# A spectral layer's four filters: row tiles, wider moving operands and more result buffers

## The chip, the cores and the metric

The kernel runs on one core of a Trainium2 chip. A core has a matrix engine (TensorE, PE in the profile, with its weight loads listed apart as PEld), a vector engine (VectorE, DVE), a scalar engine (ScalarE, ACT), a general engine (GpSimd, POOL) and a queue engine (SyncE, SP). The metric is the device time in microseconds, the median of several runs, lower is better. One further execution was recorded by the hardware profiler; every duration in this text comes from that record.

## The reference, cut to what matters

The program sends eight images of 64 x 64 points with 96 channels through four layers. The first three are state-space layers (two of the selective kind, one chunked) and take most of the time. The change is in the fourth, the spectral layer:

```
xu = upsample(x)                      # 64x64 -> 128x128, a low-pass filter along h and along w
h  = xu @ W1.T + b1                   # 96 -> 384, at each of 128*128 points
h  = coef0 + coef1*h + coef2*h*h
h  = h @ W2.T + b2                    # 384 -> 96
out = lowpass(h)[:, :, ::2, ::2]      # 128x128 -> 64x64, along h and along w
x  = x + out                          # x goes in through a group norm
```

Both filters are products of one matrix along h and the same matrix along w: `up` (64 to 128) and `down` (128 to 64). All arithmetic is in float32.

## The kernel before, in words

The eight images are worked off one after the other by the loop at the end of the program. For each one, three layers are run, and then `spectral_layer` (called in the last line of that loop). This function has five stages, each of which needs all of the one before it:

1. **Turn in.** `xs` (96 channels by 4096 points) is loaded in four pieces, GpSimd applies the group norm into `xn` (L1101), and 64 transposes (L1108), one for each row h, put w on the partitions. VectorE copies four rows at a time to `xt` (L1111), 64 partitions.
2. **Up along w.** For each of the 96 channels one matmul (L1116) has `xt[:, :, c]` as its stationary operand (64 partitions, 64 columns, 384 bytes from column to column) and `up` as its moving operand (64 rows, 128 columns). Four channels share a PSUM bank; VectorE (L1121) and ScalarE (L1119) empty the banks in turn into `x1`: h on 64 partitions, then 128 places of w, then channels.
3. **The main loop**, 32 iterations of four places of w each. Four matmuls go up along h (L1130: stationary `x1[:, w, :]`, 64 rows by 96 columns, moving `up`, 128 columns). ScalarE copies the result to `x2` (L1132), three matmuls apply W1 (L1136, 512 moving columns), ScalarE and VectorE form the polynomial (L1139, L1146), twelve matmuls apply W2 (L1153: a contiguous stationary block of 128 x 128, 96 moving columns), and VectorE adds the bias into `g` (L1160), which has h on 128 partitions.
4. **Down along h.** For each channel one matmul (L1169) with the stationary operand `g[:, :, c]`, 128 rows by 128 columns, 384 bytes from column to column, and the moving operand `down`, 64 columns. Eight channels fill a bank; VectorE (L1174) and ScalarE (L1172) empty the banks in turn into `g2`.
5. **Turn out.** For each of 16 tiles of four rows: one matmul goes down along w (L1178), four transposes bring the layer's input back (L1181), ScalarE copies these to `res` (L1185), VectorE adds the matmul (L1186), and SP writes `res` to HBM (L1187). `res` has two buffers, so the copy for tile n waits until the write of tile n-2 has landed.

A float32 matmul stands in the trace as two weight loads and two matmul records; a transpose as one of each. Within a stage a scheduler of the framework decides the order of instructions on each engine: matmuls of the next iterations' L1130 are threaded between L1136 and L1153, so that a group of L1130 can be cut into pieces. The state-space layers have orders written out by hand and are not touched. The next image starts with transposes (L1223) of a tile `tok` that is loaded (L1217) into memory which the spectral layer has used, so these loads are issued after its last transposes.

## Time and profile before

| | us |
|---|---|
| median of 3 runs (lowest, highest) | 31217.13 (31208.32, 31267.33) |
| the profiled execution's own time | 31126.95 |
| its span, first to last instruction | 31125.2 |
| PE busy, share of the span | 24477.4 (79%) |
| DVE busy | 24790.2 (80%) |
| POOL busy | 21609.0 (69%) |
| ACT busy | 16342.4 (53%) |

The last image's spectral layer, by stage, from the timeline:

| stage | from | to | us |
|---|---|---|---|
| turn in, from the first transpose | 30799.69 | 30809.55 | 9.9 |
| up along w | 30809.55 | 30831.53 | 22.0 |
| main loop | 30832.62 | 31049.21 | 216.6 |
| down along h | 31049.96 | 31091.95 | 42.0 |
| turn out, to the end of the span | 31091.75 | 31125.2 | 33.5 |

How to read the profile: a group's row gives busy time, the mean ns of one instruction, and after the second bar the time that the engine sat idle before it, with what ended the wait. Matmuls overlap, so the mean of one is longer than the distance from one to the next. A shape such as 64*128 before the tile sizes is rows by columns of the stationary operand. PEclk is the clock that was granted to TensorE, as a share of full speed; in this trace it is 1.00 or 0.50 at any moment.

### The profile page before, as it was taken

What the parts mean: (1) busy time and instruction counts of PE and PEld (TensorE: products, weight loads), DVE (VectorE), ACT (ScalarE), POOL (GpSimd) and SP (SyncE); (2) the same over time, 40 slices, a digit from 0 to 9 for tenths busy, and PEclk for the clock granted to TensorE, in tenths of its full rate; (3) what the DMA queues carried; (4) which work ended last, traced back from release to release, by engine and by line L of the source; (5) the groups of instructions that cost most, each with busy time, mean ns of one, the idle gap of its engine ahead of it and who ended that gap; (6) DMA issues with size and microseconds to landing.
All of it is one profiled execution on the core that took longest, in us unless ns stands there. A gap on an engine that the chain in (4) does not pass through costs nothing. (4 is left out here: it accounts for less than half of the span.)

```text
span 31125.2 us, 279248 instructions
## 1 busy us (share of the span) xinstructions
PE 24477.4 (79%) x90246; PEld 9300.6 (30%) x90246; DVE 24790.2 (80%) x17921; ACT 16342.4 (53%) x28493; POOL 21609.0 (69%) x8844
## 2 busy tenths in 40 slices
PE   7797877978779787797877978779787797877978
PEld 1241422414225132241412414124141241412414
DVE  9859688596885968859698596985969859698596
ACT  5536455364553645536455364653646536465364
POOL 8739487395873958739587394973948739487394
PEclk7777776777777777777777777777777777776777
DMA  5315253052530525305253152531525315253152
GB/s 124 90 24 131 64 120 92 23 133 64 119 93 21 131 67 120 92 23 132 64 122 89 25 132 63 123 88 28 133 59 123 88 27 132 60 123 88 27 132 62
DMA packets 1503971, 2689.39 MB, mean 86 GB/s; under 512 B 305624, under 2 KB 313144, under 8 KB 1502512
## 3 DMA queue, kind: packets, MB, share of 16 engines
q1 hardware_dynamic: 1485872, 2665.23, 36.6%
q8 instruction: 722, 11.83, 0.2%
q10 hardware_dynamic: 16640, 6.29, 0.1%
q14 instruction: 737, 6.04, 0.1%
HBM read 2287.51 MB, written 383.06 MB: 86 GB/s over the span
## 5 line engine op out<-in xcount | busy, mean ns | idle before, releaser
L569 DVE TENSOR_TENSOR_SCAN h<-da,db 128x1026 f32<-128x1026 f32 x6144 | 13727.8, 2280 | 513.0 <-PE py L607 173.9
L590 POOL TENSOR_TENSOR h<-h,c 128x2048 f32<-128x2048 f32 x3072 | 12755.2, 4183 | 148.4 <-ACT state L585 144.5
L533 PE MATMUL pu<-du,cst 32*128 32x512 f32 x4096 | 3239.1, 881 | 3525.3 <-DVE db L539 3493.7
L554 ACT ACTIVATE da<-dx,a0s 128x512 f32<-128x512 f32 x6144 | 4235.3, 690 | 2600.4 <-DVE h L569 2440.4
L554 ACT ACTIVATE da<-dx,a2s 128x512 f32<-128x512 f32 x6144 | 4234.5, 690 | 2591.4 <-DVE h L569 2432.0
L607 PE MATMUL py<-h,cst 128*32 128x512 f32 x24576 | 5432.2, 814 | 68.3 <-POOL h L590 68.0
L539 POOL TENSOR_TENSOR db<-du,b 128x2048 f32<-128x2048 f32 x1024 | 4657.7, 4549 | 580.8 <-ACT db L525 580.8
L539 DVE TENSOR_TENSOR db<-pu,b 128x2048 f32<-128x2048 f32 x2048 | 4637.4, 2264 | 6.3 <-issue 6.3
L607 PEld LDWEIGHTS py<-h,cst 128*32 128x32 f32 x24576 | 1182.6, 145 | 4982.1 <-issue 4505.5
L533 PEld LDWEIGHTS pu<-du,cst 32*128 32x128 f32 x4096 | 802.3, 243 | 5542.4 <-DVE db L539 3998.6
L229 POOL TENSOR_SCALAR xn<-xs,sb 96x512 f32<-96x512 f32 x192 | 208.0, 1088 | 3179.8 <-DVE sb L209 3038.8
L455 PE MATMUL pv<-u,wk 96*128 96x512 f32 x2048 | 1765.1, 1003 | 759.0 <-ACT raw L451 759.0
L952 ACT ACTIVATE sg<-sg 128x768 f32<-128x768 f32 x1024 | 819.2, 800 | 2422.4 <-PE sg L936 2422.4
L883 POOL TENSOR_TENSOR rr<-lr,cc 128x768 f32<-128x768 f32 x256 | 435.9, 1703 | 2266.9 <-ACT lr L881 1177.4
L446 PE MATMUL pv<-u,wk 96*96 96x512 f32 x2048 | 1475.4, 849 | 501.1 <-ACT state L585 239.4
L597 PE MATMUL py<-y,cst 96*96 96x512 f32 x1536 | 1551.2, 1108 | 394.6 <-ACT raw L460 356.7
L498 POOL TENSOR_TENSOR du<-raw,u 96x512 f32<-96x512 f32 x1024 | 1445.7, 1438 | 0.0
L984 DVE TENSOR_TENSOR wt<-wt,cbm 128x768 f32<-128x768 f32 x1024 | 1091.0, 1085 | 344.5 <-ACT wt L953 341.2
L585 ACT COPY state<-h 128x4 f32<-128x4 f32 x3072 | 604.6, 197 | 1163.9 <-DVE h L569 1163.8
L1022 PE MATMUL py<-wt,xdt 128*32 128x128 f32 x12288 | 1017.0, 331 | 233.2 <-DVE y L1060 155.0
L1146 DVE SCALAR_TENSOR_TENSOR f<-p,w3bs,f 128x512 f32<-128x512 f32 x768 | 576.4, 751 | 718.6 <-ACT f L1139 691.8
L1030 PE MATMUL py<-ce,state 96*96 96x128 f32 x3968 | 1115.4, 371 | 0.0
(210 smaller groups left out, 32236.4 us busy)
## 6 DMA issues: line engine op xcount, KB each, us to landing
dx<-dd SPq DMA_DIRECT2D x4096, 192.0 KB, 3.8
b<-bcd SPq DMA_DIRECT2D x2048, 256.0 KB, 5.2
c<-bcd SPq DMA_DIRECT2D x2048, 256.0 KB, 6.5
du<-dud SPq DMA_DIRECT2D x2048, 128.0 KB, 2.7
dd<-raw SPq DMA_DIRECT2D x1024, 192.0 KB, 5.3
dud<-du SPq DMA_DIRECT2D x512, 128.0 KB, 1.9
xd<-xs SPq DMA_DIRECT2D x256, 192.0 KB, 2.1
xs<-xd SPq DMA_DIRECT2D x128, 384.0 KB, 5.8
```

The costliest lines, as they stand in the source:

```text
L446: nc.tensor.matmul(pv[:DM], weights[k][:, hi, 128:], uv[hi], start=(hi == 0), stop=(hi == 1))
L455: nc.tensor.matmul(pv, weights[k][:, hi, :128], uv[hi], start=(hi == 0), stop=(hi == 1))
L498: nc.gpsimd.tensor_mul(cut(du[:, hf, :], wh), cut(delta[hf], wh), uv[hf])
L533: nc.tensor.matmul(pu, sel[rows, :], m["du"][rows, n // 3, :], start=True, stop=True)
L539: (nc.gpsimd if pool else nc.vector).tensor_mul(groups(m["db", n]), (m["du2"][:, n // 3, :] if pool else m["pu"]) .unsqueeze(1) .to_broadc ...
L554: nc.scalar.activation(dst[:, g, :LC], made[i]["dx"][n // 3][:, n % 3, :], AF.Exp, scale=av4[:, k, n, gs : gs + 1],)
L569: nc.vector.tensor_tensor_scan(made[i]["h", n][:, at][:, way], das[p][:, rev : 2 * SEG + rev][:, way], made[i]["db", n][:, at][:, way], 0. ...
L590: nc.gpsimd.tensor_mul(h, h, made[i]["c"])
L597: nc.tensor.matmul(py, skip[:, hf, :] if k == 0 else ident[:DM, :DM], view((u if k == 0 else y)[:, hf, :], wh, c * LC, LC), start=True, st ...
L607: nc.tensor.matmul(py[32 * q : 32 * q + 32, :], red, hs[q][:, g, :], start=False, stop=(g == NSG - 1),)
L984: nc.vector.tensor_mul(it["wt"], it["wt"], m["cbm"][:, j : j + 1, :].to_broadcast([128, RK, Q]),)
L1030: nc.tensor.matmul(py[:, i, hf, :], it["before"][:, 96 * hf : 96 * hf + 96], m["ce"][:, j, :], start=False, stop=True,)
```

## The change

- **Turn in.** Each transpose takes 128 points (its own row and the next), so that `xt` has 128 partitions, of which the upper 64 hold the next row. `xn` gets 64 more columns of zeros for the last one.
- **Up along w.** The moving operand is `up0`: 128 rows, the lower 64 `up` and the upper 64 zero, so the product is the same. `x1` becomes 128 partitions by 64 places: w from 0 to 63 on partitions 0 to 63, w from 64 to 127 on partitions 64 to 127. Each PSUM bank is emptied in two halves, VectorE the first and ScalarE the second; in the built program ScalarE's half waits for VectorE's.
- **Up along h.** The loop takes places 4n of the lower half and 64+4n of the upper half as a pair. Their eight matmuls alternate between rows 0 to 63 and rows 64 to 127 of the array, into two PSUM tiles out of three. The table of constants holds `up` twice, once for each half of the partitions.
- **Down along h.** The moving operand is `down2`, `down` written twice, 128 columns; the second half of the product is not used. A bank holds four channels instead of eight, and there are 24 copies of 256 elements instead of 12 of 512.
- **Turn out.** `res` has five buffers instead of two.

```diff
-            up, down = filters[:64, :128], filters[:, 128:]
-            xn = lp.tile([DM, L], F32, name="xn")
-            xt = lp.tile([64, 64, DM], F32, name="xt", tag="turn")
-            x1 = lp.tile([64, 128, DM], F32, name="x1")
+            up, down = filters[:, :128], filters[:, 128:]
+
+            down2 = lp.tile([128, 2, 64], F32, name="down2")
+            nc.gpsimd.tensor_copy(down2, down.unsqueeze(1).to_broadcast([128, 2, 64]))
+            up0 = lp.tile([128, 128], F32, name="up0")
+            nc.gpsimd.memset(up0[64:], 0.0)
+            nc.gpsimd.tensor_copy(up0[:64], up[:64])
+            xn = lp.tile([DM, L + 64], F32, name="xn")
+            nc.gpsimd.memset(xn[:, L:], 0.0)
+
+            xt = lp.tile([128, 64, DM], F32, name="xt", tag="turn")
+
+            x1 = lp.tile([128, 64, DM], F32, name="x1")
...
-                    pt = pp.tile([64, 4, DM], F32, name="pt", tag="t")
+                    pt = pp.tile([128, 4, DM], F32, name="pt", tag="t")
                     for i in range(4):
                         nc.tensor.transpose(
-                            pt[:, i, :], xn[:, (h0 + i) * 64 : (h0 + i) * 64 + 64], ident[:DM, :DM]
+                            pt[:, i, :], xn[:, (h0 + i) * 64 : (h0 + i) * 64 + 128], ident[:DM, :DM]
                         )
...
-                        nc.tensor.matmul(pt[:, i, :], xt[:, :, c0 + i], up, start=True, stop=True)
+                        nc.tensor.matmul(pt[:, i, :], xt[:, :, c0 + i], up0, start=True, stop=True)
                     dv = x1[:, :, c0 : c0 + 4].rearrange("p w c -> p c w")
-                    if c0 % 8:
-                        nc.scalar.copy(dv, pt)
-                    else:
-                        nc.vector.tensor_copy(dv, pt)
+                    nc.vector.tensor_copy(dv[:64], pt[:, :, :64])
+                    nc.scalar.copy(dv[64:], pt[:, :, 64:])
...
-                for w0_ in range(0, 128, 4):
-
-                    p2 = pp.tile([DM, 4, 128], F32, name="p2")
-                    for i in range(4):
-                        nc.tensor.matmul(p2[:, i, :], x1[:, w0_ + i, :], up, start=True, stop=True)
+                for n in range(32):
+                    w0_ = 4 * (n // 2) + 64 * (n % 2)
+                    if n % 2 == 0:
+
+                        p2s = [pp.tile([DM, 4, 128], F32, name="p2", bufs=3) for _ in range(2)]
+                        for i in range(4):
+                            for j in range(2):
+                                rows = slice(64 * j, 64 * j + 64)
+                                nc.tensor.matmul(
+                                    p2s[j][:, i, :],
+                                    x1[rows, w0_ + i, :],
+                                    up[rows],
+                                    start=True,
+                                    stop=True,
+                                )
+                    p2 = p2s[n % 2]
...
-                for c0 in range(0, DM, 8):
-                    p5 = pp.tile([128, 8, 64], F32, name="p5")
-                    for i in range(8):
-                        nc.tensor.matmul(p5[:, i, :], g[:, :, c0 + i], down, start=True, stop=True)
-                    dv = g2[:, :, c0 : c0 + 8].rearrange("p h c -> p c h")
-                    if c0 % 16:
-                        nc.scalar.copy(dv, p5)
+                for c0 in range(0, DM, 4):
+                    p5 = pp.tile([128, 4, 2, 64], F32, name="p5")
+                    for i in range(4):
+                        nc.tensor.matmul(
+                            p5[:, i, :, :], g[:, :, c0 + i], down2, start=True, stop=True
+                        )
+                    dv = g2[:, :, c0 : c0 + 4].rearrange("p h c -> p c h")
+                    if c0 % 8:
+                        nc.scalar.copy(dv, p5[:, :, 0, :])
                     else:
-                        nc.vector.tensor_copy(dv, p5)
+                        nc.vector.tensor_copy(dv, p5[:, :, 0, :])
...
-                    res = sp.tile([64, 4, DM], F32, name="res")
+                    res = rp.tile([64, 4, DM], F32, name="res")
...
-    c[:64, K_UP : K_UP + 128] = 2 * low_up[:, ::2].T
+    c[:, K_UP : K_UP + 128] = np.tile(2 * low_up[:, ::2].T, (2, 1))
```

(`rp` is a new pool, `spec4`, with five buffers.)

More of the change, by code (lines that the diff above doesn't have):

```diff
@@ L1162, in spectral_layer @@
                     )
-            with tc.tile_pool(name="ps2", bufs=3, space=PSUM) as pp:
+            with (
+                tc.tile_pool(name="ps2", bufs=3, space=PSUM) as pp,
+                tc.tile_pool(name="spec4", bufs=5) as rp,
+            ):
                 g2 = lp.tile([128, 64, DM], F32, name="g2", tag="turn")
-                for c0 in range(0, DM, 8):
-                    p5 = pp.tile([128, 8, 64], F32, name="p5")
-                    for i in range(8):
-                        nc.tensor.matmul(p5[:, i, :], g[:, :, c0 + i], down, start=True, stop=True)
-                    dv = g2[:, :, c0 : c0 + 8].rearrange("p h c -> p c h")
-                    if c0 % 16:
-                        nc.scalar.copy(dv, p5)
+                for c0 in range(0, DM, 4):
[7 more added lines that the diff above has]
+                        nc.scalar.copy(dv, p5[:, :, 0, :])
                     else:
-                        nc.vector.tensor_copy(dv, p5)
+                        nc.vector.tensor_copy(dv, p5[:, :, 0, :])
                 for h0 in range(0, 64, 4):
```

## The prediction

> **What bounds the kernel now.** I read first where the changed lines stand: the groups by line put the lines of `spectral_layer` in eight stretches of 325 to 345 us, one per image, about 8.6% of the span; nothing else can gain or lose directly. Then the stretch table of the last image (length; busy time and count of PE, PEld, DVE, ACT, POOL; granted clock; DMA share; GB/s):

> ```profile
> 30799.70:30804.00 4.30, 4.30 (x27) 4.30 (x28) 2.98 (x6) 0.00 (x0) 4.30 (x6) 0.50 0.49 122
> 30809.60:30831.50 21.90, 21.90 (x192) 21.73 (x192) 12.10 (x12) 11.07 (x11) 0.00 (x0) 1.00 0.00 1
> 30832.60:30839.70 7.10, 7.08 (x21) 4.74 (x22) 0.75 (x1) 1.94 (x3) 0.00 (x0) 0.52 0.00 0
> 30839.70:31049.20 209.50, 207.92 (x1197) 150.42 (x1195) 88.60 (x126) 90.52 (x125) 0.00 (x0) 1.00 0.00 1
> 31051.40:31091.70 40.30, 40.30 (x187) 40.30 (x187) 6.08 (x6) 5.11 (x5) 0.00 (x0) 0.50 0.00 0
> ```

> PE fills every stage up to the turn out, DVE and ACT are half idle: PE's pace is the layer's pace, and the clock is part of it. The down stage runs at half clock; so does the start of the main loop. The timeline shows that up along w has two speeds:

> ```profile
> 3596.60 40.12 PE L1116 MATMUL pt<-filters,xt 64*64 64x128 f32 x192 [1.34 <-DVE xt L1111]
> 11397.97 21.98 PE L1116 MATMUL pt<-filters,xt 64*64 64x128 f32 x192 [1.34 <-DVE xt L1111]
> ```

> Over the eight images: 40.1, 40.2, 22.0, 22.0, 22.0, 39.9, 38.9, 22.0; mean 30.9 us. Third, single lines. In two short windows of full clock, the strided weight load of L1169 and the contiguous one of L1153, both 128x128, and in another two row groups side by side in an untouched layer:

> ```profile
> L1169 PEld LDWEIGHTS p<-filters,g x6: 292/310/310, 31049.9 to 31051.0; 128*128 128x128 f32 x6
> L1153 PEld LDWEIGHTS p<-w3bs,f x362: 186/192/193, 3700.2 to 3799.3; 128*128 128x128 f32 x181
> L936 PE MATMUL sg<-rr,lr x8: 481/481/585, 5998.1 to 5999.1; 32*128 32x384 f32 x8
> ```

> L1169's loads start every 0.217 us (six in 1.1 us) at full clock, and the stage keeps 42.0/192 = 0.218 at half clock: the load sets that pace, not the matmul. L936's eight records of 384 columns, 0.32 us each if alone, all start within 1.1 us: two rows of four. Last, the turn out waits for its own writes:

> ```profile
> 31110.85 0.47 ACT L1185 COPY res<-p 64x384 f32<-64x384 f32 x1 [2.21 <-DMA out_dram<-res]
> 31111.56 0.47 ACT L1185 COPY res<-p 64x384 f32<-64x384 f32 x1 [0.23 <-DMA out_dram<-res]
> ```

> **Durations.** L1136's records of 512 columns follow at 0.43 us at full and 0.85 at half clock (its weight loads at 30850.55, 30850.98; 30837.03, 30837.88). So streaming takes 0.84 or 1.67 ns a column: 128 columns 0.107 or 0.213, 96 columns 0.080 or 0.160, 64 columns 0.054 or 0.107 us.

> [...] L1116 agrees (64 strided columns load in 193 ns, as long as L1153's 128). [...] a block of six L1130 records takes 0.83 us, where 6 x 0.11 is 0.66.

> **The change, per image.**

> *Turn in.* At half clock a transpose now loads 128 columns (0.213) and streams 96 (0.160): 64 x 0.213 = 13.6 us, plus 0.9 to the last copy, 14.5; before, first transpose to first L1116 took 9.66 on average, set by DVE's 16 copies of 0.557. Its share is 0.160/0.213 x 0.75 = 0.56, which I take as not waking. Loss 4.8. If it wakes, DVE sets the pace again and the loss is about 1. The GpSimd sets and copies stand before `xn`, where GpSimd is idle, or end under the transposes: nothing; uncovered, 128 columns cost under 0.77 (L1101's 512).

> *Up along w.* 128 rows, streaming 0.213 of 0.213: wakes within one or two windows, on average after 4.3 us, 20 records; the other 172 at 0.1145 give 19.7. Together 24.0 against 30.9: gain 6.9. The two half copies: L1121's 512 elements took 1.02; taking 0.15 as fixed, 256 take 0.58, ACT the same, 1.2 in series but spread over four banks, period 0.91: hidden. ACT's last copy now waits for DVE's: loss 0.4.

> *Start of the main loop.* Sixteen L1130 and six L1136 records at half clock took 3.5 + 4.7 us; at full clock 1.75 + 2.6. The array now arrives awake: gain 4.0.

> *Pairs.* In a cycle of four iterations L1130's five blocks take 1.47 + 0.83 + 0.60 + 0.83 + 0.60 = 4.33 us, 6.5 for six iterations. In the built order of the new kernel six iterations have five blocks. Counting neighbours of different halves as one step of 0.22, they have 4, 3, 1, 3 and 4 steps (the scheduler leaves some matmuls of one half in a row): 15 x 0.22 + 5 x 0.17 = 4.15. With 0.35 for fewer cuts in L1153, 2.7 in six iterations, 14 in 32. Bounds: 0 without overlap, 16. ACT has 2.9 us of work in an iteration of some 6: it does not become the bound.

> *Down along h.* Streaming is 0.107 under a load of 0.217, hidden; at half clock 0.213, hidden too. Pace stays, 41.7 us. The share is now 0.49 at full clock: it keeps it, which shows only later. Bounds: if load and stream did not overlap, +10; if the pace were the stream's, 192 x 0.115 = 22, a gain of 20. I take +0.4 for the shorter last copy.

> *Turn out.* From the first L1181 to the next image's L1223: 33.8 us on average (last image 33.5 to the end). Where no write is waited for, a tile takes 1.24 us of PE. With five buffers a write has 6.2 us, it needs 3.9 from copy to landing (0.5 + 0.6 + 0.6 + 2.2): no wait. Last transposes after some 20.2; then `tok` is issued and lands 5.8 later (median 5.3, 5.8 in the first image): 26.3. Gain 7.5, last image 20.2 + 1.6 + 0.6 + 2.2 = 24.7, gain 8.8. What was late because of writes is next late because of `tok`.

> Sum: 8 x (-4.8 + 6.9 - 0.4 + 4.0 + 14 + 0.4) = 161, and 61 from the turn out: **222 us**. Against the profiled execution's own time 31126.95 that is 30905.

> The median of the runs shown is 90 above that execution. Four of its images went up along w awake; were all eight asleep, it would be 72 more. If runs differ by this, the new kernel, which has one speed there, does not carry the difference; if by something else, it carries 90. I take the middle, 42: **30947**.

> **Rivals.**
> (1) *The down stage halves.* If the 0.217 belongs to the half-empty stream, 128 columns give 22 us: 20 x 8 = 160 more, 30787. Against it: the pace is the same at both clocks and the load itself lasts 310 ns.
> (2) *No overlap in the pairs*, by [...] a new wait in the scheduler's order: the 112 fall to about 0, 31059. Against it: L936.
> (3) *The transposes wake the array*: +30, 30917; inside my range.
> (4) *Slower: the main loop falls asleep.* Paired row tiles might count as 64 rows. Its stretch at full clock has PE busy 99%, and half clock would double it: the gain of 222/8 = 28 us is gone when work of 28 us in each main loop runs asleep; all 198 asleep would be 8 x 198 = 1584 more than the forecast, 32531. Against it: L1136 and L1153 alone give (2.58 x 0.75 + 24 x 0.080)/6.2 = 0.62, far above what puts to sleep.

> **How the numbers follow.** A change below 0.2%, 62 us, is about what a measurement of this kernel can't tell from none. My forecast with (3): 0.68, from 30850 to 31040. (1) 0.12; (2) 0.10; (4) 0.05; gains that cancel to near nothing 0.05. The range must reach (1) and (2): 30780 to 31095. Faster 0.90 (forecast, 1, 2), same 0.05, slower 0.05.

> **What would show it.** After the change the row of L1116's successor should have 24 us in every image with the clock at 0.50 for its first few us; the transposes 13.6 us at 0.50 (right) or under 11 with a rise (wrong); the paired matmuls two records starting together, main loop about 198 us; down 41.7 us at clock 1.00 (a figure near 22 would refute the strided load); no wait of ACT on `out_dram`, and L1223's successor waiting for a DMA. The forecast fails if the pairs run in series or the down stage is bound by something else.

## The result, and the profile after

The median went from 31212.72 us (four runs) to 30974.42 us (four runs): 238 us less, ratio 0.9926 with a 95% interval of 0.9908 to 0.9943. A second comparison, made later beside the kernel before, gave 31133.32 and 30939.07 us, ratio 0.9940 (0.9923 to 0.9957). The forecast was 30947 us. (One of the timed runs of a kernel shown below, "g for contiguous loads", took 38871 us at a mean granted clock of 0.65 instead of 0.74 and is left out of its median.) The sum is close; two of its terms were far off in opposite directions, which only the stages show.

The profiled execution took 30955.91 us (span 30953.8). The stretch table of its last image, with the same columns as the one of the kernel before (start and end; length; busy time and count of PE, PEld, DVE, ACT, POOL; granted clock; DMA share; GB/s). The six rows are turn in, up along w, start of the main loop, the rest of it, down along h, turn out:

```profile
30646.40:30655.70 9.30, 7.90 (x65) 7.24 (x65) 7.92 (x16) 0.00 (x0) 5.65 (x9) 0.81 0.22 58
30655.70:30677.70 22.00, 21.95 (x192) 21.76 (x192) 13.44 (x24) 13.04 (x23) 0.00 (x0) 1.00 0.01 1
30679.00:30686.10 7.10, 7.03 (x39) 4.13 (x40) 2.60 (x4) 4.26 (x7) 0.00 (x0) 1.00 0.00 0
30686.10:30886.70 200.60, 192.78 (x1179) 136.69 (x1178) 86.78 (x125) 88.07 (x122) 0.00 (x0) 1.00 0.00 1
30887.50:30929.90 42.40, 42.40 (x195) 42.40 (x196) 7.12 (x12) 6.49 (x12) 0.00 (x0) 1.00 0.01 1
30929.90:30953.80 23.90, 19.60 (x96) 7.82 (x93) 8.75 (x16) 7.98 (x17) 0.00 (x0) 1.00 0.28 67
```

The clock rises within the transposes, 3.7 us after the first, and from there it is full (1.00) to the end of the layer. In the 200.6 us of the main loop PE is busy 192.78: it now idles 7.8 us, where before it idled 1.6 in 209.5. Down along h takes its 42.4 us at full clock too.

The stages of all eight images, from the first record of a stage to that of the next, as means over the images (the gain is before minus after, times eight; the forecast's sums stand beside it):

| stage | before, us per image | after | gain x 8 | forecast x 8 |
|---|---|---|---|---|
| turn in | 9.67 | 9.88 | -2 | -38 |
| up along w | 30.87 | 21.95 | +71 | +55 |
| gap to the main loop | 1.10 | 1.28 | -1 | -3 |
| main loop | 217.04 | 207.72 | +75 | +144 |
| down along h, with the gap before it | 42.53 | 43.03 | -4 | +3 |
| turn out | 33.70 | 26.17 | +60 | +61 |
| the layer | 334.91 | 310.02 | +199 | +222 |

Outside the layer the two executions differ by 28 us the other way (28446 and 28474). Nothing in the changed lines touches that time; below it is seen to vary between executions of one kernel.

Single lines answer to those of before. In the timeline, the turn in and up along w of the second image:

```profile
7452.31 8.09 PE L1117 MATMUL pt<-cst,xn 96*128 96x96 f32 x64 [5.40 <-POOL xn L1110]
7461.80 21.95 PE L1125 MATMUL pt<-up,xt 128*64 128x128 f32 x192 [1.40 <-DVE xt L1120]
```

The 64 transposes take 8.1 us here and 7.9 to 8.9 over the images, not 13.6. The line view of the transposes and of the strided load of down along h, first image (durations are smallest, median, largest in ns):

```profile
L1117 PE MATMUL pt<-cst,xn x64: 246/364/419, 3572.6 to 3581.1; 96*128 96x96 f32 x64
...
L1190 PEld LDWEIGHTS p<-down,g x189: 292/313/313, 3814.4 to 3855.7; 128*128 128x128 f32 x189
```

And the timeline of ACT in the last turn out, with the wait of the next image's first transpose from the list of waits of the first turn out:

```profile
30947.23 0.47 ACT L1208 COPY res<-p 64x384 f32<-64x384 f32 x1 [0.77 <-PE p L1204]
30948.47 0.47 ACT L1208 COPY res<-p 64x384 f32<-64x384 f32 x1 [0.77 <-PE p L1204]
30949.71 0.47 ACT L1208 COPY res<-p 64x384 f32<-64x384 f32 x1 [0.77 <-PE p L1204]
...
PE pt L1246 <- DMA tok<-in_x_dram: 6.2, 1, 6.2
```

The copies come every 1.24 us and wait for PE, never for a write; in the first turn out PE then waits 6.2 us for `tok`. This is the forecast's picture of the turn out.

**Where the main loop's gain went.** The groups by line of PE, for one main loop of the kernel before (an image whose up along w was at full clock), then of the kernel after. After the bar stands idle time just before the group, and what ended it:

```profile
L1153 PE MATMUL p<-w3bs,f 128*128 128x96 f32 x768 | 100.9, 276 | 1.2 <-DVE f L1146 1.0
L1136 PE MATMUL p<-x,w3as 96*128 96x512 f32 x192 | 97.6, 619 | 0.3 <-ACT x L1132 0.3
L1130 PE MATMUL p<-filters,x 64*96 64x128 f32 x256 | 38.4, 289 | 1.1 <-ACT x L1119 1.1
```

```profile
L1171 PE MATMUL p<-w3bs,f 128*128 128x96 f32 x768 | 99.5, 276 | 6.8 <-DVE f L1164 6.3
L1154 PE MATMUL p<-x,w3as 96*128 96x512 f32 x192 | 95.5, 606 | 1.1 <-ACT x L1150 0.7
L1141 PE MATMUL p<-filters,x 64*96 64x128 f32 x256 | 23.5, 283 | 1.3 <-ACT x L1128 1.3
```

Up along h is 15 us shorter on PE (part of that is the clock at its start, 0.52 before and 1.00 after), and W2 now waits 6.3 us for `f`, the polynomial's result, which it multiplies. The timeline of PE shows one such place:

```profile
3704.68 1.05 PE L1154 MATMUL p<-x,w3as 96*128 96x512 f32 x2
3705.56 0.58 PE L1171 MATMUL p<-w3bs,f 128*128 128x96 f32 x4
3706.08 0.90 PE L1141 MATMUL p<-filters,x 64*96 64x128 f32 x12
3707.38 2.47 PE L1171 MATMUL p<-w3bs,f 128*128 128x96 f32 x20 [0.41 <-DVE f L1164]
```

L1154's last matmul makes the third part of `f` possible; ScalarE (0.78 us) and VectorE (0.75 us) must work on it before the twenty records of L1171 can run. In between PE has only four records of W2 and the paired block. The block is shorter than it was, by just the overlap that was wanted, and so PE arrives 0.41 us too early. The twelve L1141 records take up 0.9 us here; twelve at 0.11 would have taken 1.3.

### The profile page after: what moved, and what is told of

It is laid out like the page before. It is cut to its first block, busy times and chain, and to the rows that moved or that the text cites. A ratio compares the mean times of both kernels' runs of the same rounds, so it can differ in the third digit from the quotient of the medians.

```text
span 30953.8 us, 279486 instructions
## 1 busy us (share of the span) xinstructions
PE 24269.9 (78%) x90246; PEld 9118.0 (29%) x90246; DVE 24825.8 (80%) x18065; ACT 16387.8 (53%) x28637; POOL 21617.7 (70%) x8876
## 5 line engine op out<-in xcount | busy, mean ns | idle before, releaser
L455 PEld LDWEIGHTS pv<-u,wk 96*128 96x128 f32 x2048 | 534.9, 289 | 1918.2 <-ACT raw L451 1442.4
## 6 DMA issues: line engine op xcount, KB each, us to landing
b<-bcd SPq DMA_DIRECT2D x2048, 256.0 KB, 5.2
c<-bcd SPq DMA_DIRECT2D x2048, 256.0 KB, 6.5
```

Source lines behind the costliest of these rows:

```text
L455: nc.tensor.matmul(pv, weights[k][:, hi, :128], uv[hi], start=(hi == 0), stop=(hi == 1))
```

## The experiments

For each main loop I give below what a line's records *own*: the time from a record's start to the next record's start, without the idle time between them, added up. This counts overlapped records once.

**Pairs undone.** Only up along h is changed back; the scheduler orders it anew.

```
-    p2s = [pp.tile([DM, 4, 128], F32, name="p2", bufs=3) for _ in range(2)]   (for n % 2 == 0)
-    for i in range(4):
-        for j in range(2): matmul(p2s[j][:, i, :], x1[64*j:64*j+64, w0_ + i, :], up[64*j:64*j+64])
+    rows = slice(64 * (n % 2), 64 * (n % 2) + 64)
+    p2 = pp.tile([DM, 4, 128], F32, name="p2", bufs=2)
+    for i in range(4):
+        matmul(p2[:, i, :], x1[rows, 4 * (n // 2) + i, :], up[rows])
```

> Pairs alone undone: each tile's four up-along-h matmuls stand together again, on its own 64 rows, with two p2 buffers as before; all else as in the changed kernel. Theory (W: the pairs save some 11 us of TensorE in each main loop, and 6.3 us of that come back as a wait for f): the L1141 records own 34 instead of 23.1 us, TensorE's idle time in the main loop falls from 7.8 to under 2 us, the loop goes from 207.7 to about 213, the whole kernel about 40 us slower than the changed one. Rival (A: row tiles overlap only a little on the array, the wait is an accident): the idle time stays near 7.8, the loop grows by what the array saved alone. Second rival (N: the pairs save nothing, all of the loop's gain was the clock): loop 207.7, no difference.

Measured: 30925.61 us, ratio to the kernel before 0.9928 (0.9912 to 0.9944), as good as the changed kernel's. The main loop took 209.4 us in four images and 210.9 to 214.3 in the four in which the clock fell to one half about 2 us after its start, for 3.4 to 10.2 us (in the profiles of both kernels every stretch at one clock lasts a window of 3.413 us or a whole number of them; one at half clock is a "lost window" from here on); mean 210.8 against 207.7. The groups of PE in the first main loop:

```profile
L1163 PE MATMUL p<-w3bs,f 128*128 128x96 f32 x762 | 100.3, 276 | 2.1 <-DVE f L1156 1.0
L1146 PE MATMUL p<-x,w3as 96*128 96x512 f32 x192 | 95.7, 608 | 0.5 <-ACT x L1142 0.5
L1138 PE MATMUL p<-filters,x 64*96 64x128 f32 x256 | 30.8, 288 | 1.3 <-ACT x L1128 1.3
```

The wait for `f` falls from 6.3 to 1.0 us, as theory W wanted, and PE's idle time from 7.8 to 2.7. But the L1138 records own only 29.2 us, not 34: even without pairs, some of their time is gone. In the trace, where the block of one tile (rows 0 to 63) ends and that of the next (rows 64 to 127) begins, the two overlap by themselves. The blocks stand in the same order as in the kernel before, of 12, 6, 4, 6 and 4 records; but one of 12 owns 1.19 us instead of 1.48, and one of 6 owns 0.60 or 0.67 instead of 0.82. So the pairs as written are worth 6.0 us on PE and lose 5.2 of them to idle time; with a change of 0.8 in W1 and W2 together, 1.7 us a loop remain, less than a measurement of the whole can see. (Summed over the images with the lost windows, the layer took 2504 us instead of 2480; outside the layer this execution happened to spend 62 us less.)

**The order written by hand.** The same work; the order of the main loop is written out instead of left to the scheduler.

```
+    fa = first(xa)                       # first: W1 and f of a tile; second: W2 and bias
+    for k in range(16):
+        fb = first(xb)
+        if k < 15:
+            p2s = rows_up(k + 1)         # eight matmuls, halves alternating
+            xa = to_sbuf(p2s[0])
+        second(fa, 4 * k)
+        if k < 15:
+            xb = to_sbuf(p2s[1])
+            fa = first(xa)
+        second(fb, 4 * k + 64)
```

> Same work as in the changed kernel, but the main loop's order is written out by hand: W1 of one tile always stands between the W1 of the tile before and that tile's W2, and eight paired matmuls, strictly alternating, follow each second W1. So f has a whole W1 (2.6 us) more to be ready. Theory W: no wait for f is left; 192 x 0.43 + 768 x 0.112 = 168.5 us, 16 blocks of 8 x 0.11 + 0.17 = 16.8, some 8 for changes between lines as now, 2 for the start: about 195 us instead of 207.7, the whole kernel about 100 us faster than the changed one. Rival A (overlap is limited by the array): the wait goes, but the paired blocks own more than 20 us again and the loop stays above 201. Rival S (the scheduler's order is not what costs; the wait only moves to x2 or p3): idle time stays above 5 us, loop within 2 us of 207.7.

Measured: 30826.06 us, ratio 0.9897 (0.9876 to 0.9918). The main loop took 189.2 us, or 190.9 to 192.4 in three images that lost one or two windows; mean 190.2, which is 17.6 us less than after. Theory W had put it at about 195. The groups of PE and its timeline:

```profile
L1177 PE MATMUL p<-w3bs,f 128*128 128x96 f32 x761 | 90.7, 276 | 0.0
L1158 PE MATMUL p<-x,w3as 96*128 96x512 f32 x192 | 88.6, 598 | 0.7 <-ACT x L1151 0.7
L1140 PE MATMUL p<-filters,x 64*96 64x128 f32 x256 | 17.9, 279 | 1.3 <-ACT x L1128 1.3
```

```profile
3684.82 2.82 PE L1177 MATMUL p<-w3bs,f 128*128 128x96 f32 x24
3687.48 2.77 PE L1158 MATMUL p<-x,w3as 96*128 96x512 f32 x6
3690.17 1.12 PE L1140 MATMUL p<-filters,x 64*96 64x128 f32 x16
3691.22 2.92 PE L1177 MATMUL p<-w3bs,f 128*128 128x96 f32 x24
```

No wait for `f` is left. Of the 18.5 us between 207.7 and 189.2, 7.1 are idle time, 6.3 are L1140 (23.1 to 16.8 owned), and 2.6 and 2.5 are W1 and W2, which are no longer cut into pieces of one and two records. Rivals A and S fall.

**The same order, halves not alternating.**

```
-    for i in range(4):
-        for j in range(2):
+    for j in range(2):
+        for i in range(4):
```

> The hand-written order of the run before it, but in each block the four matmuls of the first row half stand together, then the four of the second: no neighbour is of another half, except at the change. Theory W: overlap is lost, 16 blocks grow by 8 x 0.11 less one overlap, about 0.85 us each, so the loop is 13 to 15 us longer than with alternating halves (about 209), the whole kernel some 110 us slower than that. Rival A: difference of 5 us a loop or less. Together with the run before it this gives the pairs' own worth with no wait in the way.

Measured: 30860.17 us, ratio 0.9904 (0.9889 to 0.9919); loop 196.9 us where no window was lost, 7.7 more than with alternating halves. The up along h lines own 25.0 instead of 16.8, which is 8.2 more, and 0.5 of idle time is gone. 7.7 is between the theory's 13 to 15 and rival A's 5; the whole kernel is 34 us slower than with alternating halves, not 110. The starts of the sixteen records of one block, in us from its first, in the order in which each half was issued (the two halves are told apart by their own even steps of 0.109):

```
rows 0 to 63:    0     0.186 0.296 0.405 0.514 0.623 0.732 0.841
rows 64 to 127:  0.520 0.706 0.816 0.925 1.034 1.143 1.252 1.361
```

The first record of the second half starts while the first half still has three to go. So TensorE took work of the other half three to four records early: neighbours need not alternate to overlap, here it was enough that they lay within that reach. That is also part of why undoing the pairs cost so little.

**g for contiguous loads.** The array that down along h loads is turned round.

```
-    g = lp.tile([128, 128, DM], F32, name="g")
+    g = lp.tile([128, DM, 128], F32, name="g")
...
-    g[:, w0_ : w0_ + 4, :], p4, ...
+    g[:, :, w0_ : w0_ + 4].rearrange("p c w -> p w c"), p4, ...
...
-    nc.tensor.matmul(p5[:, i, :, :], g[:, :, c0 + i], down2, ...)
+    nc.tensor.matmul(p5[:, i, :, :], g[:, c0 + i, :], down2, ...)
```

> The changed kernel with g laid out so that the 128 elements which a down-along-h weight load reads in a partition stand next to one another (g is [128, channel, w]); the bias add writes it with a stride instead. Theory (L: the strided load sets the down stage's pace): a record every 0.112 us as with the contiguous loads of L1171, stage 192 x 0.112 = 21.5 and some start: about 22 instead of 42.45 us, 8 x 20 = 160 us faster than the changed kernel. Rival (P: a stream of 128 columns whose half is thrown away, or the copies out of PSUM, set the pace): stage stays at 42. Cost to look for: the bias add (0.56 us) may take up to twice as long with strided writes; DVE has 2.8 us of work in 6.5 us, so the main loop should stay within 2 us of 207.7, unless the add stands in f's way.

Measured: 30781.18 us (three runs), ratio 0.9878 (0.9859 to 0.9896). Down along h takes 21.68 us in every image instead of 42.45. The load in the line view:

```profile
L1192 PEld LDWEIGHTS p<-down,g x192: 187/192/192, 3815.8 to 3837.1; 128*128 128x128 f32 x192
```

192 ns instead of 313, a record every 0.112 us instead of 0.220, with the same shape, the same moving operand and the same copies behind it. So the stride of the load set that stage's pace; the moving operand and the copies did not. For the kernel before this is inferred: its loads (310 ns) and its pace (0.218 us) are nearly the same, and the run with 64 columns below repeats them. The price is the bias add, 813 ns instead of 558 on average, and it is hidden: the loop stays at 207.7 us (two images lost one or two windows).

**The padding undone.**

```
-    nc.tensor.matmul(pt[:, i, :], xt[:, :, c0 + i], up0, ...)
+    nc.tensor.matmul(pt[:, i, :], xt[:64, :, c0 + i], up[:64], ...)
```

> The changed kernel with only the padding undone: up along w multiplies xt[:64] (64 rows) again, its transposes still load 128 columns, copies and pairs stay. Theory (K: a stream on 64 rows, share 0.47 to 0.50, can keep the clock but cannot win it back): as in the kernel before, two speeds, about 22 us in images that arrive awake and stay so, about 40 in the others; between two and six of the eight are slow, and those also start the main loop at half clock: 9 to 13 us an image on average, 50 to 120 us in all slower than the changed kernel. Rival (T: it is the wider transposes that brought the clock, the padding does nothing): 21.95 us at clock 1.00 in all eight images, no difference.

Measured: 31059.09 us, ratio 0.9975 (0.9964 to 0.9987). The two speeds are back, four images of each. From the timeline:

```profile
3578.41 21.98 PE L1125 MATMUL pt<-filters,xt 64*64 64x128 f32 x192 [1.31 <-DVE xt L1120]
11315.07 40.18 PE L1125 MATMUL pt<-filters,xt 64*64 64x128 f32 x192 [1.31 <-DVE xt L1120]
```

In all eight images the clock rose to full during the transposes. Where it rose late in them (6.0 to 6.8 us after the first) it lasted through the stage; where it rose early (3.7 to 4.4 us) it was gone again 6.8 us later, just after the seam between transposes and L1125 (1.3 us without a matmul), and the 64 rows did not bring it back in the 40 us of the stage. In all eight the main loop began at half clock (210.6 to 211.5 us instead of 207.7). The profile of the kernel before shows the same: in its four slow images the clock rose 3.7 to 5.8 us after the first transpose, stayed full for 6.8 us and fell 1.3 to 2.8 us after the first record of L1116. Over the eight images the padding is worth 72 us in the stage and 26 in the main loop, within the 50 to 120 that theory K gave; rival T falls.

**64 columns down along h, and two result buffers.**

```
-    p5 = pp.tile([128, 4, 2, 64], F32, name="p5")        # moving operand down2
+    p5 = pp.tile([128, 4, 64], F32, name="p5")           # moving operand down
```

> The changed kernel with down along h on 64 moving columns again (four matmuls to a PSUM tile, the whole tile copied). Theory (L, the load sets the pace): stage 42 to 42.5 us as with 128 columns, but the clock falls to 0.50 within two windows of its start; the turn out starts at half clock and wins it back after one or two windows: last transposes 2 to 4 us later than +20.0, and as the last write and then tok wait for them, the turn out goes from 26.2 to 28 to 30; 15 to 30 us in all. Rival (H: the 128 columns gain nothing): turn out stays at 26.2, no difference to be seen in the stages.

```
-    tc.tile_pool(name="spec4", bufs=5) as rp,
+    tc.tile_pool(name="spec4", bufs=2) as rp,
```

> The changed kernel with two res buffers instead of five. Theory (B: a buffer's write has not landed when its turn comes): ACT's copies wait for the write again, turn out 33.7 instead of 26.2 us, 24.2 to 33 in the last image: 7.5 x 7 + 8.8 = 61 us slower. Rival (C: the turn out gained because it now starts awake, not through the buffers): turn out stays below 28.

Measured with 64 columns: 30922.06 us, ratio 0.9932 (0.9914 to 0.9949), no difference from the changed kernel in the whole. Its stretch table for down along h and for the turn out of the first image:

```profile
3821.10:3862.50 41.40, 41.40 (x192) 41.12 (x192) 7.03 (x12) 7.54 (x13) 0.00 (x0) 0.52 0.00 1
3862.70:3890.00 27.30, 20.99 (x97) 9.01 (x96) 8.74 (x16) 7.44 (x16) 0.00 (x0) 0.88 0.48 115
```

The clock column falls to 0.52 and the stage takes 42.0 us as before: the wide operand keeps the clock (1.00 with it) and gains nothing in its own stage (42.45 us with it). The turn out is 27.7 instead of 26.2 us, less than the 28 to 30 that I had expected: 12 us in all, of which the wide operand gives back 4 in its own stage.

Measured with two buffers: 30987.78 us, ratio 0.9946 (0.9926 to 0.9965). The turn out is 32.0 us on average, and in the first image's list of waits the writes are back:

```profile
ACT res L1208 <- DMA out_dram<-res: 21.1, 13, 4.2
```

So the five buffers are worth 256.0 - 209.3 = 47 us over the eight images; the other 13 of the turn out's 60 us came with the clock, which is full there from the start. That agrees with the 12 us that the run with 64 columns lost, with five buffers and a start at half clock.

**Both improvements.** The hand-written order and the turned `g` together.

> Both at once: main loop in the hand-written order and g laid out for contiguous weight loads. Theory: the two are in different stages and add: main loop 189 to 191, down 21.7, all other stages as in the changed kernel; against the changed kernel 8 x (17.5 + 20.8) less some for the strided bias add = 300 us faster, ratio to the kernel before about 0.983. Rival: the strided bias add (0.56 us before; it may be slower) delays p4 or f in the tighter order: TensorE idles over 3 us in the loop and it stays above 193.

Measured: 30663.88 us, ratio 0.9844 (0.9825 to 0.9863), the fastest kernel here. Main loop 189.2 to 192.3 us (mean 191.4; seven images lost one or two windows), down along h 21.7, the other stages as after. The layer takes 2183 us over the eight images instead of 2480: 297 us less, where the two gains alone, 140 and 162, add up to 302. The rival falls: PE idles 0.7 us in the loop, and the slower bias add delays nothing.

**Both kernels once more.**

> The kernel before, unchanged, profiled once more. The prediction put the 90 us between its profiled execution and its median half down to the clock: in that execution four of eight images went up along w awake, and were all asleep it would be 72 us more. Theory (C): the number of slow images changes between executions, and the time outside the spectral layer stays within 20 us of 28446. Rival (O): four of eight again (or three to five), and the difference between executions lies outside the layer, by 30 us or more.

> The changed kernel, unchanged, profiled and timed once more beside the kernel before. Theory: its stages repeat to 0.1 us except for single clock windows (main loop 207.7 to 211, turn in 9.3 to 10.3), 2480 us in the eight images; what differs between executions lies outside the layer. Ratio to the kernel before 0.991 to 0.994. Rival: the stages themselves differ by more than 10 us in sum.

The kernel before took 31093.92 us; three of its eight images were slow instead of four, and 28428 us lay outside the layer, 18 less than the first time. The kernel after took 30925.58 us in its profiled execution: 2484 us in the layer (2480 the first time; one image lost two windows) and 28440 outside, 34 less. So the stages repeat to 4 us in sum, and a difference of 30 us outside the layer means nothing. One slow image less and the 18 us fit theory C, but three slow images were within the rival's bounds too, and the other kernel's 34 us are more than the 20 of theory C. Whether the number of slow images is what spreads the executions of the kernel before over 100 us (31093 to 31192; 24 us for the kernel after beside it) stays open: kernels with one speed there, as the hand-written order, spread over 78 us too. In both kernels, longer runs had the lower mean granted clock (0.732 at 31093 us and 0.730 at 31192; 0.738 at 30793 and 0.736 at 30871), so the spread goes with the clock; in which stages, these runs don't show.

## Why the prediction was right or wrong

**Turn in: wrong.** The step that failed is "a transpose now loads 128 columns (0.213) and streams 96 (0.160): 64 x 0.213". I priced the load like a stream, 1.67 ns a column at half clock. In the trace the transposes follow every 0.160 us at half and every 0.083 us at full clock: about the pace of the 96 columns that stream, at both, and the same as in the kernel before, whose loads had 64 columns. The weight loads of the first image, in the kernel before and after (the largest figures are from half clock, the smallest from full):

```profile
L1108 PEld LDWEIGHTS pt<-cst,xn x64: 108/112/177, 3587.3 to 3594.9; 96*64 96x64 f32 x64
L1117 PEld LDWEIGHTS pt<-cst,xn x64: 138/226/229, 3572.6 to 3581.0; 96*128 96x128 f32 x64
```

The load did get longer, but it overlaps its neighbours (226 ns, a record every 0.160 us) and doesn't set the pace. So the share of streaming stays 0.75, which by my own criterion wakes the clock, and it did after 3.7 to 6.9 us in every image: rival (3), priced at 30 us; it gave 36. (The criterion, streaming time times rows, with its bounds of 0.57 and 0.75, was my estimate from the stages of the kernel before; what the clock goes by is not shown.) The number of columns alone did not set the time of a load or the pace: with 128 columns at full clock a record came every 0.083 us for a transpose (load 140 ns), 0.112 for a float32 matmul (192 ns), 0.220 for one with a stride (313 ns).

**Up along w: right, mis-sized.** It gained 8.9 us an image, not 6.9, because the array arrives awake, at full clock (1.00 through the stage in all eight images); the one or two windows at half clock in the forecast, 4.3 us, were my estimate, and none was spent. The padding is the cause: without it the two speeds return (21.98 and 40.18 us in the two images shown). DVE's and ACT's halved copies (583 and 579 ns each) are hidden, as said; the gap grew by 0.2, not 0.4.

**Start of the main loop: right.** With the padding undone, a start at half clock cost 3.2 us a loop in the paired kernel; the forecast, for the kernel before, was 4.0.

**Pairs: wrong.** The forecast was 14 us an image; beyond the 4.0 of the start 5.3 came. The overlap itself was right: records start 7 ns apart, 0.109 us from pair to pair, and L1141 owns 23.1 us where the working gives 4.15 x 32/6 = 22.1. What failed is the sentence "ACT has 2.9 us of work in an iteration of some 6: it does not become the bound". ScalarE did not become the bound, but I counted the busy time of the engines and not the chain from W1 over ScalarE and VectorE to W2, and so put a new wait for `f` at nothing. The L1130 block had been the filler that hid this chain; shortened, it leaves 0.41 us uncovered every second iteration, 6.3 us in all: a new wait.

In numbers, for the image of the kernel before whose groups are shown, with the 1.75 and 2.1 us of its slow start taken off: up along h goes from 34.0 to 23.1 us owned, 10.9 gained where the working has 34.7 to 22.1, 12.6; W1 and W2 together go from 177.1 to 176.7, 0.4 instead of the 1.9 that "0.35 for fewer cuts" comes to; idle time grows from 1.6 to 7.9 and takes 6.3. That leaves 5.0. Of these the pairing itself gives only 1.7, what its undoing cost; the other 3.3 come from tiles that alternate between the two row halves, and stay without it.

The hand-written order shows what the same pairs can give where the chain is covered. Rival (2), no overlap, is refuted by the same records. The new wait from the scheduler's order, of which it spoke too, is what happened, with the overlap intact.

**Down along h: right.** The stage stayed at 42 us and the clock stayed full (one image lost a window). Rival (1), that it halves with the wide operand, is refuted; it halves with a contiguous load. The runs show that contiguity doubles the pace (0.220 to 0.112 us a record), not why: no other stride was tried.

**Turn out: right** to 1 us of 61, though not by buffers alone: 47 of it are theirs, 13 the clock's.

**Slower by a sleeping main loop: did not happen.** The clock was 1.00 through all eight loops; in the second profile one loop lost two windows.

**The level.** The working put 30905 against the profiled execution and 42 more for the median. The profiled execution came out at 30956: 23 of the difference are the stages, 28 lie outside the layer. The median lies 18 above the profiled execution, not 42. The forecast of 30947 is 27 below the median. That it came so close is luck: +36 (turn in), +16 (up along w) and -69 (main loop) nearly cancel.

## What to carry to other kernels

Before shortening a block of work, ask what it was covering: the chain W1, ScalarE, VectorE, W2 needs some 1.7 us here from the end of W1's last record, and once the filler between them was shorter than that, what was saved became a wait, though ScalarE and VectorE were under half busy. The order then has to change with it (here one more W1 before each W2: 18 us of 208). And look at how a weight load walks through memory before widening what streams past it: one change of layout took 20 us off a stage of 42, and the wide operand none.

## What the runs showed of the hardware that was not expected

- The load of 128 columns for a transpose did not hold up a stream of 0.083 us a record (0.160 at half clock), while contiguous loads for float32 matmuls followed at 0.112. Loads with 384 bytes from column to column came every 0.218 us at half and 0.220 us at full clock, and took 310 to 313 ns each.
- Records of another row half were started early by three to four places: with four matmuls of each half in a row, the second half began 0.52 us into a block in which the first ran 0.95. Strict alternation made a block of sixteen records own 1.05 us, halves one after the other 1.56.
- With the padding undone, whether 64 gapless rows kept the full clock went with the place in the transposes where it had risen: at 6.0 to 6.8 us it lasted, at 3.7 to 4.4 it was lost. In the two profiles of the kernel before the line between is narrow (5.81 us lost, 5.91 lasted), and a rise at 9.27 us was lost too. With 128 rows it lasted through the stage in every image of every run. Why the seam decides is not shown.
- VectorE's bias add took 813 instead of 558 ns when it wrote its 384 elements with a stride.
